# Deformable convolution, attention and experts on one core: the mean as one more column, the variance by ScalarE's squares, the output's bias added in DRAM

## The chip, the core and the metric

The kernel runs on one core of a Trainium2 chip. The metric is the device time in microseconds (us) of one execution. Five engines work side by side, each through its own queue in order: TensorE (PE in the profile, PEld its weight loads), VectorE (DVE), ScalarE (ACT), GpSimd (POOL) and SyncE (SP), which here only issues DMAs. GpSimd issues the indirect DMAs, and the one DMA that adds to what it finds in DRAM.

## The reference, cut to what matters

The input is `x[4, 256, 64, 64]`; a token is one of the 4096 pixels of one of the four images, with 256 channels.

```python
x = x + L0_conv(_gn(x), ...)            # deformable 3x3 convolution, with a residual
t = _to_tokens(x)
t = t + L1_attn(_ln_t(t), ...)          # attention over the four images; its output is o @ Wo + bo
t = t + L1_ffn(_ln_t(t), ...)           # 8 experts, the best two of a token by softmax(tokens @ router_w.T)
# _ln_t: (v - mean) / sqrt(var + 1e-5), over the 256 channels of a token
```

The attention's scores are sums over all positions, one 4x4 matrix for each of 8 heads; so they are complete only after every token has been read once.

## The kernel before, in words

Four stages follow one another.

- **Convolution** (from 0 to about 1862 us of the profiled span). For each tile of 128 pixels and each of 9 taps GpSimd gathers corners (L519), ScalarE and VectorE weigh them (L535, L543), TensorE turns and multiplies them (L557, L582). A finished row of the result `acc` has CR = 264 columns: 256 channels and 8 router columns (`NE`), the product of the row with the router's weights, since the convolution's weights have been multiplied by the router beforehand (`routed`). ScalarE copies it to `o`, and a DMA writes 4 tiles at a time to `t1[b][j]` in DRAM: image b, block j of 512 tokens, 8 blocks.
- **Scores** (to about 2181 us). For j in 8 blocks, for b in 4 images: SP loads `bt<-t` (L739, 4 tiles of 128 tokens, three buffers), `layernorm` (L184, L185 statistics, L170 variance plus epsilon, L176 the power -0.5 on GpSimd, L188 the result), TensorE turns it (L675) and projects q and k (L686), ScalarE copies them (L744, L752), VectorE multiplies every pair of images (L759, 32 instructions in each block). The compiler's scheduler orders this stage.
- **Mixing and routing** (to about 2611 us). Function `block(j)` writes out an order by hand, and TensorE, VectorE and ScalarE keep it; GpSimd's own order is fixed by the dependencies that `in_turn` adds between its powers and its scatters. For each block: `value` and `mixed` (L686, L869, L876) weigh the value projections of the four images; `gate` (L686, ScalarE's sigmoid L881), `gated` (L898), `output` (L908, 264 columns, eight of them for the router), `residual` (DMA `dt<-t` L892 and the bias added by VectorE L893), `added` (L922 the channels, L924 the router's columns), `stats` (L935, L937, then L172 and the power L176), `shift` (L948, minus the mean times 1/sigma), `normed` (L955, L960 on ScalarE, into the tile `u`), `pick` (L973 to L991, the best two experts), `count`, `placed` (L1018 to L1030, the `slots` of each token) and `scatter` (L1039, one indirect DMA for each 128 rows, 32 for a block).
- **Experts** (to the end), with the results gathered back and added.

Within `block(j)` the end of one block and the start of the next interlock. The last of block j-1 is `shift(j-1, 3)`, then `pick`, `count`, `placed`; then come `scatter(14)` of block j-1, the power of `stats(j, 0)`, `scatter(4)`, the power of `stats(j, 1)`, `scatter(4)`, the power of `stats(j, 2)`, `scatter(5)`, the power of `stats(j, 3)`, and the remaining five scatters. The call in `stats` that fixes this on GpSimd is

```python
            in_turn(issued[-1], scattered)
            scattered.clear()
```

On ScalarE the order at the end of a block is: sigmoids of image 2, sigmoids of image 3, `normed` of images 0, 1 and 2, the eight products of the next block's `value`, `normed` of image 3.

Of the kernel before, what the change touches and what calls it, by code (L numbers as in the profile page):

```python
# [9 lines left out]
F32 = mybir.dt.float32  # L10
# [7 lines left out]
P = 128  # L18
# [11 lines left out]
NE = 8  # L30


CR = C + NE
BLK = 512
NT = BLK // P
RB = BLK // W
# [33 lines left out]
def conv_attn_moe_kernel(  # L70
# [60 lines left out]
    def load_weight(pool, ap, name):  # L131
        t = pool.tile([P, NCH, ap.shape[1]], F32, name=name)
        nc.sync.dma_start(t, ap.rearrange("(ch p) o -> p ch o", p=P))
        return t

    def routed(rows, rw, ps_turned, ps_out, pool, name):


        pr = ps_out.tile([P, len(rows), NE], F32, name=f"{name}_pr", tag="om")
        for n, w in enumerate(rows):  # L140
            tp = ps_turned.tile([P, C], F32, name=f"{name}_tp{n}", tag="tp")
            for ch in range(NCH):
                T.transpose(tp[:, ch * P : (ch + 1) * P], w[:, ch * P : (ch + 1) * P], ident)
            wT = pool.tile([P, C], F32, name=f"{name}_wT{n}", tag="sT")
            S.copy(wT, tp)
            for ch in range(NCH):
                T.matmul(
                    pr[:, n, :], wT[:, ch * P : (ch + 1) * P], rw[:, ch, :],
                    start=(ch == 0), stop=(ch == NCH - 1),
                )  # L150
        for n, w in enumerate(rows):
            V.tensor_copy(w[:, C:], pr[:, n, :])
# [9 lines left out]
                reason="order of issue",  # L162
            )

    def rstd_of(pool, var, n, name, twice=False, into=None):


        ve = pool.tile([P, n], F32, name=f"{name}_ve", tag=f"ve{n}")
        if twice:
            V.tensor_scalar(ve, var, 1.0 + EPS, EPS * EPS, ALU.mult, ALU.add)  # L170
        else:
            V.tensor_scalar(ve, var, EPS, None, ALU.add)  # L172
        r = into
        if into is None:
            r = pool.tile([P, n], F32, name=f"{name}_rstd", tag=f"rstd{n}")
        issued.append(G.tensor_tensor(r, ve, nhalf[:, :n], ALU.pow))  # L176
        return r

# [23 lines left out]
    with ExitStack() as actx:  # L202
# [48 lines left out]
        wconv_sb = aw.tile([P, NCH, K2, CR], F32, name="wconv_sb")  # L251
        for ch in range(NCH):
            nc.sync.dma_start(wconv_sb[:, ch, :, :C], w_conv[ch * P : (ch + 1) * P])
        rwc_sb = load_weight(aw, router_w, "rwc_sb")


        zeros = aw.tile([P, 4 * C], F32, name="zeros")
# [436 lines left out]
    dw = wctx.enter_context(tc.tile_pool(name="d_w", bufs=1))  # L694
    wv_sb = load_weight(dw, wv, "wv_sb")
    wg_sb = load_weight(dw, wg, "wg_sb")
    rw_sb = load_weight(dw, router_w, "rw_sb")
    wo_sb = dw.tile([P, NCH, CR], F32, name="wo_sb")
    nc.sync.dma_start(wo_sb[:, :, :C], wo.rearrange("(ch p) o -> p ch o", p=P))
    bo_sb = dw.tile([P, CR], F32, name="bo_sb")  # L700
# [5 lines left out]
    with ExitStack() as bctx:  # L706
        bw = bctx.enter_context(tc.tile_pool(name="b_w", bufs=1))
        bt = bctx.enter_context(tc.tile_pool(name="b_t", bufs=3))
        bs = bctx.enter_context(tc.tile_pool(name="b_s", bufs=2))
        bqk = bctx.enter_context(tc.tile_pool(name="b_qk", bufs=2 * B + 3))  # L710
        ps_tp = bctx.enter_context(tc.tile_pool(name="ps_tpb", bufs=3, space=PSUM))
        ps_mm = bctx.enter_context(tc.tile_pool(name="ps_mmb", bufs=4, space=PSUM))

        wq_sb = load_weight(bw, wq, "wq_sb")
        wk_sb = load_weight(bw, wk, "wk_sb")
        with ExitStack() as ectx:
            et = ectx.enter_context(tc.tile_pool(name="e_t", bufs=1))
            ps_e = ectx.enter_context(tc.tile_pool(name="ps_e", bufs=1, space=PSUM))
            routed([wo_sb[:, ch, :] for ch in range(NCH)], rw_sb, ps_tp, ps_e, et, "wo")

            alike = et.tile([P, NCH, P], F32, name="alike")
            V.tensor_copy(alike, bo_c.unsqueeze(2).to_broadcast([P, NCH, P]))
            pb = ps_e.tile([P, 2, NE], F32, name="pb", tag="om")
            for n in range(2):
                for ch in range(NCH):
                    T.matmul(
                        pb[:, n, :], alike[:, ch, :] if n == 0 else ones, rw_sb[:, ch, :],
                        start=(ch == 0), stop=(ch == NCH - 1),
                    )
            V.tensor_copy(bo_sb[:, C:], pb[:, 0, :])  # L730
            V.tensor_copy(rsum, pb[:, 1, :])
        head_sum = block_diagonal(bw, "head_sum", DHEAD, 1.0)
        parts = bw.tile([P, NCH, B * B, NBLK], F32, name="parts")

        for j in range(NBLK):
            qs, ks = [], []
            for b in range(B):
                rows = bt.tile([P, NT, CR], F32, name=f"bt{b}_{j}", tag="t")
                nc.sync.dma_start(rows, t1[b][j])  # L739
                t = rows[:, :, :C]  # L740
                layernorm(bs, t, t, f"l1_{b}_{j}", twice=True)
                mn = channel_major(b, j)
                for ch, tp in transpose_in(ps_tp, t, f"tpb{b}_{j}"):
                    S.activation(  # L744
                        mn[:, ch, :], tp, AF.Identity,
                        scale=gamma_c[:, ch : ch + 1], bias=beta_c[:, ch : ch + 1],
                    )
                q = bqk.tile([P, NCH, BLK], F32, name=f"q{b}_{j}", tag="qk")
                k = bqk.tile([P, NCH, BLK], F32, name=f"k{b}_{j}", tag="qk")
                for w, dst, n in ((wq_sb, q, "q"), (wk_sb, k, "k")):  # L750
                    for ch in range(NCH):
                        S.copy(dst[:, ch, :], project(ps_mm, w, mn, ch, f"p{n}{b}_{j}_{ch}"))  # L752
                qs.append(q)
                ks.append(k)
            for s_ in range(B):
                for t_ in range(B):
                    for ch in range(NCH):
                        junk = bs.tile([P, BLK], F32, name=f"junk{s_}{t_}{ch}_{j}", tag="junk")
                        V.scalar_tensor_tensor(  # L759
                            junk, qs[s_][:, ch, :], 1.0, ks[t_][:, ch, :],  # L760
                            ALU.mult, ALU.mult,
                            accum_out=parts[:, ch, s_ * B + t_, j : j + 1],
                        )


        per_ch = bw.tile([P, NCH, B * B], F32, name="per_ch")
        V.tensor_reduce(per_ch, parts, AX.X, ALU.add)
        pl = ps_mm.tile([P, NCH * B * B], F32, name="pl", tag="mm")
        T.matmul(pl, head_sum, per_ch.rearrange("p ch n -> p (ch n)"), start=True, stop=True)
        rows = NCH * B  # L770
        lg = bw.tile([P, rows, B], F32, name="lg")
        V.tensor_scalar(lg, pl.rearrange("p (r t) -> p r t", t=B), ATT_SCALE, None, ALU.mult)
        mx = bw.tile([P, rows], F32, name="mx")
        V.tensor_reduce(mx, lg, AX.X, ALU.max)
        V.tensor_tensor(
            lg, lg, mx.unsqueeze(2).to_broadcast([P, rows, B]), ALU.subtract
        )
        S.activation(lg, lg, AF.Exp)
        V.tensor_reduce(mx, lg, AX.X, ALU.add)
        V.reciprocal(mx, mx)  # L780
        V.tensor_tensor(
            att.rearrange("p ch s t -> p (ch s) t"), lg,
            mx.unsqueeze(2).to_broadcast([P, rows, B]), ALU.mult,
        )
# [65 lines left out]
    with ExitStack() as bctx:  # L850
# [36 lines left out]
        def residual(j, b):  # L887
            for i in range(0, NT, 2):
# [1 line left out]
                    [P, 2, CR], F32, name=f"dt{b}_{j}_{i}", tag="t", bufs=4  # L890
                )
                nc.sync.dma_start(t, t1[b][j][:, i : i + 2])  # L892
                V.tensor_tensor(t, t, bo_sb.unsqueeze(1).to_broadcast([P, 2, CR]), ALU.add)  # L893

        def gated(j, b):
            o, g = os_[j, b], gs.pop((j, b))
# [16 lines left out]
        def added(j, b):  # L913
            r = token_major(b, j)
            if b == 0:
                ss[j] = bs.tile([P, NG, NE], F32, name=f"s{j}", tag="s")
                lns[j] = tuple(
                    bs.tile([P, NG], F32, name=f"{n}{j}", tag=n) for n in ("rstd", "shift")
                )
# [8 lines left out]
                nc.sync.dma_start(t2[b, j], r)  # L928

        def stats(j, b):  # L930
            x_ = token_major(b, j)
            st = bs.tile([P, NT, V.BN_STATS_DIM], F32, name=f"l3st{b}_{j}", tag="ln_st")
            mv = bs.tile([P, NT, V.BN_AGGR_DIM], F32, name=f"l3mv{b}_{j}", tag="ln_mv")
            for i in range(NT):
                V.bn_stats(st[:, i, :], x_[:, i, :])  # L935
            for i in range(NT):
                V.bn_aggr(mv[:, i, :], st[:, i, :])  # L937
            rstd_of(
                bs, mv[:, :, 1], NT, f"l3_{b}_{j}", into=lns[j][0][:, b * NT : (b + 1) * NT]
            )  # L940
            in_turn(issued[-1], scattered)
            scattered.clear()
            lns[j, b] = mv

        def shift(j, b):
            r, nb = (x[:, b * NT : (b + 1) * NT] for x in lns[j])
            mv = lns.pop((j, b))
            V.scalar_tensor_tensor(nb, mv[:, :, 0], -1.0, r, ALU.mult, ALU.mult)  # L948

        def normed(j, b):  # L950
            x_ = token_major(b, j)
            r, nb = lns[j]
            u = us[j, b] = bu.tile([P, NT, ROW], F32, name=f"u{b}_{j}", tag="u")

            S.activation(  # L955
                u[:, :, C:], place, AF.Copy, bias=float((b * HB + j % HB) * BLK)
# [10 lines left out]
        def pick(j):  # L967


            r, nb = lns.pop(j)  # L970
            lg = ss.pop(j)
            mean = bs.tile([P, NG, NE], F32, name=f"mean{j}", tag="lg", bufs=1)
            V.tensor_tensor(mean, over_tiles(rsum), over_experts(nb), ALU.mult)  # L973
            V.tensor_tensor(lg, lg, over_experts(r), ALU.mult)
# [514 lines left out]
```

## Time and profile before

| | us |
|---|---|
| median of 3 runs | 3274.14 (3273.08 to 3282.42) |
| profiled execution, its own time | 3278.02 |
| its span, first to last instruction | 3276.30 |
| busy: PE, DVE, ACT, POOL | 2972.6, 2600.0, 1722.3, 1854.4 |
| mean granted TensorE clock | 0.958 of full speed |

The profile is of one execution. Busy shares are over the whole span, in which the four stages have different limits, so the stages are read one at a time. The idle time of an engine is named by what ended it. POOL's indirect DMAs show as about 1 us of GpSimd each: that is the issue, not the transfer.

### The profile page before, as it was taken

The page shows a single profiled execution, that of the slowest core. Times are in us where ns is not written, and L with a number is a line of the kernel's source. Part 1 is how long each engine was busy: PE and PEld are TensorE (multiplying, and loading weights), DVE is VectorE, ACT ScalarE, POOL GpSimd, SP SyncE. Part 2 cuts the span into 40 slices and gives each one's busy share as a digit, 9 for nine tenths or more (in the row PEclk, how much of TensorE's full clock was granted, in tenths as well). Part 3 has the DMA queues.
Part 4 walks back from the last instruction along what each step waited for, and adds up shares of the span by engine and source line. Part 5 has one row for each costly group of instructions (what it writes and reads, how often), then busy time and mean ns, then how long its engine had stood idle before and what let it go on. Part 6 is the DMA issues. An engine that isn't in the chain of part 4 may idle for free. (4 is left out here: it accounts for less than half of the span.)

```text
span 3276.3 us, 49563 instructions
## 1 busy us (share of the span) xinstructions
PE 2972.6 (91%) x13658; PEld 2175.3 (66%) x13658; DVE 2600.0 (79%) x6611; ACT 1722.3 (53%) x3912; POOL 1854.4 (57%) x1800
## 2 busy tenths in 40 slices
PE   6889998899998899989999898978888899999995
PEld 2667776677776677767777644434444488888883
DVE  1488888878897888899999788878888766567777
ACT  3456665556664566655555444334242355556552
POOL 0377667676676767677777411105676767554440
PEclk8799999999998999999999899989999999999995
DMA  5789999999999899999999821106453445447778
GB/s 167 261 330 405 390 386 345 400 340 386 390 351 393 336 402 386 386 342 409 409 404 402 312 66 55 60 24 200 156 173 104 136 137 169 159 159 248 245 236 316
DMA packets 322182, 898.89 MB, mean 274 GB/s; under 512 B 43218, under 2 KB 89949, under 8 KB 319860
## 3 DMA queue, kind: packets, MB, share of 16 engines
q0 software_dynamic: 191808, 671.74, 53.1%
q1 hardware_dynamic: 130100, 223.98, 21.1%
q8 instruction: 113, 1.85, 0.2%
q14 instruction: 161, 1.32, 0.1%
HBM read 744.43 MB, written 154.79 MB: 274 GB/s over the span
## 5 line engine op out<-in xcount | busy, mean ns | idle before, releaser
L543 DVE SCALAR_TENSOR_TENSOR s<-g,wts,s 128x256 f32<-128x256 f32 x3456 | 1446.5, 480 | 226.4 <-ACT s L535 220.2
L519 POOL DMA_INDIRECT g<-table,idx x1152 | 1220.6, 1060 | 536.7 <-DVE s L543 279.7
L582 PE MATMUL acc<-wconv_sb,sT 128*128 128x264 f32 x4608 | 1275.2, 400 | 58.6 <-ACT sT L563 57.7
L582 PEld LDWEIGHTS acc<-wconv_sb,sT 128*128 128x128 f32 x4608 | 794.2, 192 | 186.6 <-ACT sT L563 83.9
L535 ACT ACTIVATE s<-g,wts 128x256 f32<-128x256 f32 x1152 | 587.5, 510 | 342.1 <-DMA g<-table,idx 322.4
L563 ACT COPY sT<-tps 128x256 f32<-128x256 f32 x1152 | 418.8, 364 | 352.9 <-PE tps L557 347.5
L557 PE MATMUL tps<-ident,s 128*128 128x128 f32 x2304 | 449.1, 277 | 48.6 <-DVE s L543 48.0
L557 PEld LDWEIGHTS tps<-ident,s 128*128 128x128 f32 x2304 | 316.3, 144 | 260.6 <-issue 170.9
L1313 POOL DMA_INDIRECT ys_rows<-y,to x284 | 282.7, 995 | 259.6 <-DVE y L1310 191.5
L1039 POOL DMA_INDIRECT xs_rows<-u,slots x256 | 260.6, 1018 | 126.8 <-issue 110.7
L1284 PE MATMUL ph<-xT,w 128*128 128x256 f32 x1136 | 270.8, 381 | 0.7 <-ACT hT L1288 0.6
L1302 PE MATMUL py<-w,hT 128*128 128x256 f32 x1136 | 268.4, 379 | 0.0
L1288 ACT ACTIVATE hT<-ph,w 128x256 f32<-128x256 f32 x284 | 134.4, 474 | 198.0 <-PE ph L1284 197.5
L1302 PEld LDWEIGHTS py<-w,hT 128*128 128x128 f32 x1136 | 215.8, 190 | 29.3
L1307 DVE TENSOR_TENSOR y<-py,w 128x512 f32<-128x512 f32 x142 | 98.2, 692 | 171.0 <-ACT w L1246 129.8
L1284 PEld LDWEIGHTS ph<-xT,w 128*128 128x128 f32 x1136 | 206.2, 192 | 24.1 <-ACT hT L1288 1.6
L390 PE MATMUL po<-xs,woff_sb 128*96 128x512 f32 x384 | 204.3, 628 | 0.0
L176 POOL TENSOR_TENSOR l_rstd<-l_ve,nhalf 128x4 f32<-128x4 f32 x32 | 34.4, 1075 | 253.7 <-DVE l_ve L170 253.7
L881 ACT ACTIVATE gate<-pg,bg_c 128x512 f32<-128x512 f32 x64 | 43.9, 686 | 243.0 <-PE pg L686 242.9
L759 DVE SCALAR_TENSOR_TENSOR junk<-q,k 128x512 f32<-128x512 f32 x256 | 160.9, 684 | 8.9 <-ACT k L752 8.9
L876 DVE SCALAR_TENSOR_TENSOR mix<-pv,att,mix 128x512 f32<-128x512 f32 x192 | 129.7, 742 | 1.9 <-PE pv L686 1.9
L908 PE MATMUL po<-wo_sb,mix 128*128 128x264 f32 x512 | 117.8, 386 | 0.0
(228 smaller groups left out, 3287.8 us busy)
## 6 DMA issues: line engine op xcount, KB each, us to landing
xt<-xs_rows SPq DMA_DIRECT2D x142, 260.0 KB
table<-zt SPq DMA_DIRECT2D x128, 256.0 KB
early_state<-ys_rows SPq DMA_DIRECT2D x128, 256.0 KB
g<-table,idx POOLq DMA_INDIRECT x1152, 7.8
t<-o SPq DMA_DIRECT2D x32, 528.0 KB
bt<-t SPq DMA_DIRECT2D x32, 528.0 KB
dt<-t SPq DMA_DIRECT2D x64, 264.0 KB
xraw<-in_x SPq DMA_DIRECT2D x16, 1024.0 KB
```

What stands on the lines that cost most here:

```text
L390: T.matmul(t["po"], woff_sb[:, ch, ki].rearrange("p kj o -> p (kj o)"), t["xs"][:, ch, ki : ki + RB], start=(n == 0), stop=(n == NCH * 3 - 1),
L519: g = G.indirect_dma_start(out=gs[n % NGB], out_offset=None, in_=tables[b], in_offset=bass.IndirectOffsetOnAxis(ap=params[b][0][:, r, k : ...
L535: first = S.activation(ss[n], gs[n % NGB][:, :C], AF.Copy, scale=params[b][1][:, 0, r, k : k + 1])
L543: last_corner[n] = V.scalar_tensor_tensor(ss[n], gs[n % NGB][:, c * C : (c + 1) * C], params[b][1][:, c, r, k : k + 1], ss[n], ALU.mult, A ...
L557: T.transpose(tps[n][:, ch * P : (ch + 1) * P], s[:, ch * P : (ch + 1) * P], ident)
L563: S.copy(sTs[n], tps.pop(n))
L582: T.matmul(accs[n // K2][:, :CR], sT[:, ch * P : (ch + 1) * P], wconv_sb[:, ch, k, :], start=False, stop=(k == K2 - 1 and ch == NCH - 1),)
L759: V.scalar_tensor_tensor(junk, qs[s_][:, ch, :], 1.0, ks[t_][:, ch, :], ALU.mult, ALU.mult, accum_out=parts[:, ch, s_ * B + t_, j : j + 1],)
L1039: s = G.indirect_dma_start(out=rows_, out_offset=bass.IndirectOffsetOnAxis(ap=slots[:, k, n : n + 1], axis=0), in_=u[:, n % NT, :], in_off ...
L1284: T.matmul(ph, w1_sb[:, ch, f * P : (f + 1) * P], xT[:, ch, :], start=(ch == 0), stop=(ch == NCH - 1),)
L1302: T.matmul(py[:, i, :], hT[:, f, i * P : (i + 1) * P], w2_sb[:, f, :], start=(f == 0), stop=(f == NCH - 1),)
L1313: s = G.indirect_dma_start(out=ys_rows[g], out_offset=bass.IndirectOffsetOnAxis(ap=to[:, i : i + 1], axis=0), in_=y[:, i, :], in_offset=No ...
```

## The change

The router's weights get a ninth column (`NX` = 9) filled with -1/256. A row's product with it is minus the row's mean, and it is carried wherever the eight router columns were carried: CR is 265. `stats` no longer uses VectorE's statistics: ScalarE squares each tile of 128 tokens with the carried mean as its bias and sums along the row (`accum_out`), into `u`, which `normed` overwrites later; VectorE forms variance plus epsilon from the sum. `shift` takes the mean from the ninth column. The bias `bo_sb` is no longer added by VectorE in `residual`: in the scores' loop, after a block has been loaded, GpSimd issues a DMA that adds it to `t1[b][j]` in DRAM; the load of that loop takes only the 256 channels.

```diff
-CR = C + NE
+NX = NE + 1
+CR = C + NX
...
+    def load_router(pool, name):
+        t = pool.tile([P, NCH, NX], F32, name=name)
+        G.memset(t[:, :, NE:], -1.0 / C)
+        nc.sync.dma_start(t[:, :, :NE], router_w.rearrange("(ch p) o -> p ch o", p=P))
+        return t
...
-        rwc_sb = load_weight(aw, router_w, "rwc_sb")
+        rwc_sb = load_router(aw, "rwc_sb")
...
-    rw_sb = load_weight(dw, router_w, "rw_sb")
+    rw_sb = load_router(dw, "rw_sb")
...
-                rows = bt.tile([P, NT, CR], F32, name=f"bt{b}_{j}", tag="t")
-                nc.sync.dma_start(rows, t1[b][j])
-                t = rows[:, :, :C]
+                t = bt.tile([P, NT, C], F32, name=f"bt{b}_{j}", tag="t")
+                nc.sync.dma_start(t, t1[b][j][:, :, :C])
                 layernorm(bs, t, t, f"l1_{b}_{j}", twice=True)
+                G.dma_start(
+                    t1[b][j], bo_sb.unsqueeze(1).to_broadcast([P, NT, CR]), accum_op=ALU.add
+                )
...
                 nc.sync.dma_start(t, t1[b][j][:, i : i + 2])
-                V.tensor_tensor(t, t, bo_sb.unsqueeze(1).to_broadcast([P, 2, CR]), ALU.add)
...
         def stats(j, b):
-            x_ = token_major(b, j)
-            st = bs.tile([P, NT, V.BN_STATS_DIM], F32, name=f"l3st{b}_{j}", tag="ln_st")
-            mv = bs.tile([P, NT, V.BN_AGGR_DIM], F32, name=f"l3mv{b}_{j}", tag="ln_mv")
+            x_, mean = token_major(b, j), ss[j][:, :, NE:]
+            u = us[j, b] = bu.tile([P, NT, ROW], F32, name=f"u{b}_{j}", tag="u")
+            var = bs.tile([P, NT], F32, name=f"l3var{b}_{j}", tag="var")
             for i in range(NT):
-                V.bn_stats(st[:, i, :], x_[:, i, :])
-            for i in range(NT):
-                V.bn_aggr(mv[:, i, :], st[:, i, :])
-            rstd_of(
-                bs, mv[:, :, 1], NT, f"l3_{b}_{j}", into=lns[j][0][:, b * NT : (b + 1) * NT]
+                n = b * NT + i
+                S.activation(
+                    u[:, i, :C], x_[:, i, :], AF.Square, bias=mean[:, n],
+                    accum_out=var[:, i : i + 1],
+                )
+            ve = bs.tile([P, NT], F32, name=f"l3_{b}_{j}_ve", tag=f"ve{NT}")
+            V.tensor_scalar(ve, var, 1.0 / C, EPS, ALU.mult, ALU.add)
+            issued.append(
+                G.tensor_tensor(lns[j][0][:, b * NT : (b + 1) * NT], ve, nhalf[:, :NT], ALU.pow)
             )
...
-            mv = lns.pop((j, b))
-            V.scalar_tensor_tensor(nb, mv[:, :, 0], -1.0, r, ALU.mult, ALU.mult)
+            V.tensor_tensor(nb, ss[j][:, b * NT : (b + 1) * NT, NE], r, ALU.mult)
...
-            u = us[j, b] = bu.tile([P, NT, ROW], F32, name=f"u{b}_{j}", tag="u")
+            u = us[j, b]
...
-            lg = ss.pop(j)
+            lg = ss.pop(j)[:, :, :NE]
```

Built, the changed kernel keeps the orders written by hand. On ScalarE the four squares of image 0 stand between the sigmoids of image 2 and those of image 3; the squares of images 1, 2 and 3 stand each after `normed` of the image before. On VectorE the instruction that forms the variance plus epsilon stands where it stood. On GpSimd the powers and scatters of the mixing stage stand as they stood; in the scores' stage the first two adding DMAs stand ahead of the first power, and the further ones one or two at a time between the powers.

More of the change, by code (lines that the diff above doesn't have):

```diff
@@ L134, in load_weight @@
         return t
+    def load_router(pool, name):
[3 more added lines that the diff above has]
+        return t
     def routed(rows, rw, ps_turned, ps_out, pool, name):
-        pr = ps_out.tile([P, len(rows), NE], F32, name=f"{name}_pr", tag="om")
+        pr = ps_out.tile([P, len(rows), NX], F32, name=f"{name}_pr", tag="om")
         for n, w in enumerate(rows):
@@ L163, in in_turn, with rstd_of @@
             )
-    def rstd_of(pool, var, n, name, twice=False, into=None):
+    def rstd_of(pool, var, n, name, twice=False):
         ve = pool.tile([P, n], F32, name=f"{name}_ve", tag=f"ve{n}")
@@ L172, in rstd_of @@
             V.tensor_scalar(ve, var, EPS, None, ALU.add)
-        r = into
-        if into is None:
-            r = pool.tile([P, n], F32, name=f"{name}_rstd", tag=f"rstd{n}")
+        r = pool.tile([P, n], F32, name=f"{name}_rstd", tag=f"rstd{n}")
         issued.append(G.tensor_tensor(r, ve, nhalf[:, :n], ALU.pow))
@@ L722, in conv_attn_moe_kernel @@
             V.tensor_copy(alike, bo_c.unsqueeze(2).to_broadcast([P, NCH, P]))
-            pb = ps_e.tile([P, 2, NE], F32, name="pb", tag="om")
+            pb = ps_e.tile([P, 2, NX], F32, name="pb", tag="om")
             for n in range(2):
@@ L730, in conv_attn_moe_kernel @@
             V.tensor_copy(bo_sb[:, C:], pb[:, 0, :])
-            V.tensor_copy(rsum, pb[:, 1, :])
+            V.tensor_copy(rsum, pb[:, 1, :NE])
         head_sum = block_diagonal(bw, "head_sum", DHEAD, 1.0)
@@ L915, in added @@
             if b == 0:
-                ss[j] = bs.tile([P, NG, NE], F32, name=f"s{j}", tag="s")
+                ss[j] = bs.tile([P, NG, NX], F32, name=f"s{j}", tag="s")
                 lns[j] = tuple(
@@ L942, in stats @@
             scattered.clear()
-            lns[j, b] = mv
         def shift(j, b):
             r, nb = (x[:, b * NT : (b + 1) * NT] for x in lns[j])
-            mv = lns.pop((j, b))
-            V.scalar_tensor_tensor(nb, mv[:, :, 0], -1.0, r, ALU.mult, ALU.mult)
+            V.tensor_tensor(nb, ss[j][:, b * NT : (b + 1) * NT, NE], r, ALU.mult)
         def normed(j, b):
```

## The prediction

> **What bounds the kernel now.** I read the busy time by stretches first, since the change acts in two stages. Columns: stretch, its length, busy us (and instructions) of PE, PEld, DVE, ACT and POOL, granted clock, DMA share, GB/s. The rows are the scores, the first block of mixing, the other seven blocks.
>
> ```profile
> 1870.00:2181.00 311.00, 267.48 (x779) 130.89 (x780) 259.33 (x938) 119.89 (x194) 34.91 (x35) 0.93 0.17 55
> 2181.00:2229.50 48.50, 46.18 (x135) 25.65 (x134) 38.51 (x92) 17.75 (x33) 4.17 (x3) 0.97 0.33 108
> 2229.50:2611.00 381.50, 322.87 (x932) 172.79 (x930) 324.46 (x874) 132.89 (x294) 258.03 (x244) 0.95 0.44 149
> ```
>
> No engine is full in the last row, and VectorE, at 85%, looks like the one to relieve. So I went on to the timeline of one block, for a chain that closes on itself. First GpSimd (start, length, engine, line, what it does, in brackets the idle time before it):
>
> ```profile
> 2300.90 0.95 POOL L1039 DMA_INDIRECT xs_rows<-u,slots  x1 [6.19 <-issue]
> 2302.16 0.96 POOL L1039 DMA_INDIRECT xs_rows<-u,slots  x1 [0.30 <-issue]
> ...
> 2318.59 0.96 POOL L1039 DMA_INDIRECT xs_rows<-u,slots  x1 [0.30 <-issue]
> 2319.67 1.22 POOL L176 TENSOR_TENSOR rstd<-l_ve,nhalf 128x4 f32<-128x4 f32 x1
> ...
> 2325.94 1.57 POOL L176 TENSOR_TENSOR rstd<-l_ve,nhalf 128x4 f32<-128x4 f32 x1
> ...
> 2332.60 1.22 POOL L176 TENSOR_TENSOR rstd<-l_ve,nhalf 128x4 f32<-128x4 f32 x1
> ...
> 2340.13 1.32 POOL L176 TENSOR_TENSOR rstd<-l_ve,nhalf 128x4 f32<-128x4 f32 x1
> ```
>
> Then VectorE in the same block:
>
> ```profile
> 2300.68 0.18 DVE L1030 CAST slots<-row 128x16 int32<-128x16 f32 x1
> ...
> 2319.22 0.29 DVE L172 TENSOR_SCALAR l_ve<-l3mv 128x4 f32<-128x4 f32 x1
> ...
> 2341.49 0.16 DVE L948 SCALAR_TENSOR_TENSOR shift<-l3mv,rstd 128x4 f32<-128x4 f32 x1 [0.94 <-POOL rstd L176]
> ...
> 2353.87 0.17 DVE L1030 CAST slots<-row 128x16 int32<-128x16 f32 x1
> ```
>
> The reader is to see a loop. Slots are ready at 2300.86; 14 scatters, one every 1.26 us, fill GpSimd to 2319.55; then four powers with 4, 4 and 5 scatters between them, without a gap, to 2341.45. VectorE waits for the last power, shifts, picks, mixes, and has the next slots at 2354.04. That is 40.6 us of GpSimd and 12.6 of VectorE: 53.2 us, the period of the block. VectorE is busy beside GpSimd but only 12.6 us of its work are in the loop. Its variance for the first power (L172) ends at 2319.51, 0.04 us before GpSimd is free. So an earlier variance gains nothing, a later one delays the loop.
>
> The third view is ScalarE at the end of the same block:
>
> ```profile
> 2319.18 0.69 ACT L881 ACTIVATE gate<-pg,bg_c 128x512 f32<-128x512 f32 x1 [1.03 <-PE pg L686]
> ...
> 2326.18 0.69 ACT L881 ACTIVATE gate<-pg,bg_c 128x512 f32<-128x512 f32 x1 [1.03 <-PE pg L686]
> ...
> 2326.87 2.06 ACT L960 ACTIVATE u<-early_state,shift,rstd 128x256 f32<-128x256 f32 x4
> ...
> 2336.03 4.70 ACT L869 ACTIVATE mix<-pv,att 128x512 f32<-128x512 f32 x8
> ```
>
> ScalarE is a third full, but in order: `normed` of image 0 starts only when the sigmoids of image 3 are done, and the new squares of image 1 stand behind it.
>
> **The mixing stage, blocks 1 to 7.** Removed from VectorE per block: eight adds at L893, 0.62 us apart (two in 1.24), 5 us; 16 statistics and aggregations, 1.7 us an image, 6.8 us. Of this the loop holds nothing. Two adds stand between the slots and the first power; without them VectorE, and the TensorE products that wait for its mixes, come 1.24 us earlier.
>
> Added: 16 squares on ScalarE. No row shows a square with a sum. L535, 128x256 with one operand per partition, takes 510 ns, L960 with two 588, and four L960 take 2.06, a pitch of 0.49; so a square has a pitch of 0.41. For the sum, the smallest ScalarE row (L985, four in 0.47) gives a pitch of 0.1 us. Four squares: 4 x 0.51 + 0.1, so 2.2 us; bounds 1.75 (sum free) and 3.0 (194 ns each, L985 alone, and the pitch of L960). I take 2.2, as VectorE's own read of a sum (84 ns) is nearer to the lower row. The built program has no more table loads than before (seven), so no switch is charged.
>
> Now the steps, by the block above:
> - Image 0: the sigmoids of image 2 end at 2319.87 - 1.24 = 2318.6. Squares to 2320.8, variance and hand-over 0.25, power at 2321.1 instead of 2319.67. Queued behind VectorE's waiting instruction: `gated` of image 2 and `added` of image 1.
> - Image 1: the sigmoids of image 3 end at 2325.6, `normed` of image 0 at 2327.6, squares at 2329.8, power at 2330.05 instead of 2325.94: **4.1 us late**. VectorE, done with `shift` at 2324, stands still for some 6 us, and behind it `gated` of image 3, for which TensorE waits.
> - Images 2 and 3: from power to power GpSimd needs 6.66 and 7.53 us (four and five scatters). Shift, `normed` (2.06), squares (2.2) and hand-overs need about 6.1 from power to power. GpSimd sets the pace again, with 0.5 and 1.5 us to spare, and the 4.1 us stay.
>
> With squares of 1.75 the delay is 3.7, with 3.0 it is 5.2. The next slots come as much later: nothing in the 12.6 us changed.
>
> A second cost is TensorE's clock. The eight products at L869 start behind the squares of image 3, at 2342.4, so TensorE, with three of four value projections done by 2340.5, idles to about 2344.7, some 4.2 us. After an idle time of 3.94 us the trace shows eight matmuls (L686, 512 columns) at 6.03 us, which take 3.60 later:
>
> ```profile
> 1875.98 2.19 PE L675 MATMUL tpb<-ident,bt 128*128 128x128 f32 x8 [3.94 <-DVE bt L188]
> 1878.46 6.03 PE L686 MATMUL pq<-early_state,wq_sb 128*128 128x512 f32 x8 [0.29 <-ACT early_state L744]
> 1884.32 3.60 PE L686 MATMUL pk<-early_state,wk_sb 128*128 128x512 f32 x8
> ```
>
> That is up to 2.4 us more before the products that `placed` needs, which had some 2.4 us to spare and lose about 2 of it: 0 to 2.2 us a block, I take 0.5. The Trainium skill ("TensorE: Matmul & The Clock Gate", Part 1) speaks against this change here: after an idle window of about 3.4 us the array runs at half clock for about as long again; by it the sum would have 1.7 us a block instead of 0.5, 8 us more in all.
>
> Seven blocks: 7 x (4.1 + 0.5) = 32.2 us. In block 0 nothing is scattered, and powers follow each other after 4.83 us (2225.89, 2230.72) where the new chain needs 6.0: three steps, 3.5 us. **Sum 35.7 us**; bounds 28 (3.7 a block and 2) and 56 (7.4 and 4).
>
> **The scores' stage.** GpSimd gets 32 adding DMAs. No row shows one. A gather of 128 rows costs GpSimd 1060 ns; this one has 512 rows, so 1.06 to 4.24 us, and I take 2.6, between them, as a part of the 1060 must be fixed. Two of them precede the first power and wait for `bo_sb`, written at 1872.25: with 0.3 us between issues the power moves from 1874.44 to 1878.1, 3.5 us (0.6 to 7). Later VectorE sets the pace, 36.3 us a block (powers at 1931.67 and 1967.93), and an issue fits between two powers 4.43 us apart up to 3.4 us: 0.5 us in all, at most 7. The transfer is covered: DMA share is 0.17, and GpSimd waits for the landing only eight such DMAs later. The load it follows, 540 KB, is issued at 1888.82 and used at 1892.47, 3.65 us. Read, read and write one after another make 11 us at most. I take **4 us** for the stage, 0.6 to 15. The Trainium skill ("DMA: Bandwidth & Descriptors", Anatomy of one DMA) gives 2.0 us plus bytes/436e3 for a DMA from GpSimd, 3.2 us for this one, not for one that adds; by it the transfer would be hidden even more surely.
>
> **The convolution.** One more column: 16 matmuls of 264 columns take 3.72 us, 8 of 512 take 3.60, so 0.84 ns a column, times 4608, 3.9 us if TensorE set the pace. ScalarE waited 322 us there for gathers, and DMA share is 0.97 to 1.00 between 200 and 1800 us, so most of it is covered: **1 us**, 0 to 4. The ninth column elsewhere, the memsets and the copies: nothing, a few ns each.
>
> **Sum.** 3278.0 (the profiled execution; 1.7 of it outside the span) + 35.7 + 4 + 1 = 3318.7. That execution lies 3.9 above the median, so 3315 in the median's terms, 41 us slower (1.2%).
>
> **Rivals.**
> - *VectorE sets the pace and its relief pays.* For it: 85% busy, and GpSimd waited 9.9 us for the variance in 2230 to 2611. Against: the loop above. If squares ran beside everything, 12 us a block would go, 8 x 12 = 97: 3274 - 97 + 5 = 3182; with GpSimd's loop as floor only the 9.9 and some 5 of block 0 go: 3264. It decides if the variance of image 1 is ready within 25 us of the slots, instead of 29. Chance 0.08.
> - *Squares in time, loop unchanged*: sigmoids of image 3 earlier than I have them. 3274 + 5, less a few of the 9.9: 3274. Chance 0.07.
> - *The adding DMAs become the bound of the scores' stage.* An image has 9.07 us there (36.3/4). At 11 us each, the end above, 1.9 x 32 = 61 us more: 3376, and worse beyond it. Against: DMA share 0.17. Chance 0.15.
> - The forecast: 0.70, 3296 to 3336 by itself.
>
> The range reaches from the lower bounds (3302), with some room, to part of the third rival: 3296 to 3358. The measurement can tell 0.3% (9.8 us) from no change. Faster 0.08, same 0.07, slower 0.85.
>
> **What would show it.** Right: blocks 1 to 7 some 58 to 60 us apart instead of 53 to 55; VectorE idle some 6 us ahead of the variance of image 1, put down to ScalarE; that power some 29 us behind the slots; no gap on GpSimd after it; the scores' stage longer by a few us. Wrong: GpSimd still without a gap before the second power (faster or same), squares over 0.8 us apart (block by more than 6), or GpSimd at over 4 us an adding DMA, VectorE waiting for loads or powers in the scores.

## The result, and the profile after

The change makes the kernel slower: 3303.3 us (median of four runs) against 3274.1, a ratio of 1.0084 with a 95% interval of 1.0055 to 1.0112. The forecast was 3315, in a range from 3296 to 3358. The profiled execution of the changed kernel took 3301.75 us (span 3300.0), 23.7 more than the one of before; that one lies 3.9 above its kernel's median and this one 1.5 below, so the stages below account for 23.7 us, not for the 29 between the medians.

I read the stages first, by the same instructions in both kernels. The convolution ends where GpSimd clears `head_sum`; the scores end with ScalarE's first mix; the mixing stage goes from there to the start of the last power.

| stage | predicted | before | after | difference |
|---|---|---|---|---|
| convolution | +1 | 1861.2 | 1855.8 | -5.4 |
| scores | +4 | 322.8 | 328.0 | +5.2 |
| mixing and routing | +35.7 | 431.7 | 452.1 | +20.4 |
| rest, to the end | 0 | 660.6 | 664.0 | +3.4 |

Busy time by stretches, columns as in the prediction (PE, PEld, DVE, ACT, POOL, granted clock, DMA share, GB/s), for the scores, the first block of mixing and the other seven:

```profile
1870.00:2181.00 311.00, 267.14 (x771) 129.28 (x772) 258.16 (x917) 119.83 (x194) 71.75 (x65) 0.93 0.58 105
2181.00:2229.50 48.50, 43.55 (x121) 23.77 (x120) 26.30 (x52) 21.75 (x52) 2.89 (x3) 0.92 0.29 94
2229.50:2631.00 401.50, 330.40 (x947) 182.63 (x945) 245.16 (x597) 190.05 (x521) 245.74 (x244) 0.95 0.42 143
```

VectorE was relieved as intended: in the seven blocks it is busy 245 us instead of 324. The stage is longer all the same. One block of it, as in the prediction, GpSimd first:

```profile
2361.95 0.95 POOL L1050 DMA_INDIRECT xs_rows<-u,slots  x1 [6.39 <-issue]
...
2382.02 1.34 POOL L952 TENSOR_TENSOR rstd<-l_ve,nhalf 128x4 f32<-128x4 f32 x1 [2.65 <-DVE l_ve L950]
...
2391.03 1.41 POOL L952 TENSOR_TENSOR rstd<-l_ve,nhalf 128x4 f32<-128x4 f32 x1 [2.64 <-DVE l_ve L950]
...
2397.50 1.04 POOL L952 TENSOR_TENSOR rstd<-l_ve,nhalf 128x4 f32<-128x4 f32 x1
...
2404.85 1.04 POOL L952 TENSOR_TENSOR rstd<-l_ve,nhalf 128x4 f32<-128x4 f32 x1
```

The first two powers now have a gap ahead of them, the last two have none. VectorE of the same block:

```profile
2361.73 0.17 DVE L1041 CAST slots<-row 128x16 int32<-128x16 f32 x1
...
2381.70 0.17 DVE L950 TENSOR_SCALAR l_ve<-l3var 128x4 f32<-128x4 f32 x1 [4.28 <-ACT u L945]
...
2390.78 0.17 DVE L950 TENSOR_SCALAR l_ve<-l3var 128x4 f32<-128x4 f32 x1 [6.28 <-ACT u L945]
...
2405.92 0.16 DVE L959 TENSOR_TENSOR shift<-s,rstd 128x4 f32<-128x4 f32 x1 [2.85 <-POOL rstd L952]
...
2418.41 0.17 DVE L1041 CAST slots<-row 128x16 int32<-128x16 f32 x1
```

VectorE stands still 4.28 and 6.28 us for ScalarE's squares. Why they are late is to be seen on ScalarE: the squares of image 1 (L945) stand behind the sigmoids of image 3 (L890) and `normed` of image 0 (L971).

```profile
2386.03 0.69 ACT L890 ACTIVATE gate<-pg,bg_c 128x512 f32<-128x512 f32 x1 [0.97 <-PE pg L692]
2386.61 0.20 ACT L966 ACTIVATE u<-place 128x16 f32<-128x16 f32 x1
2386.72 2.06 ACT L971 ACTIVATE u<-early_state,shift,rstd 128x256 f32<-128x256 f32 x4
2388.68 0.49 ACT L945 ACTIVATE u<-early_state,s 128x256 f32<-128x256 f32 x1
2389.08 0.19 ACT L945 ACTIVATION_READ_ACCUMULATOR u<-early_state,s 128x1 f32 x1
2389.18 0.49 ACT L945 ACTIVATE u<-early_state,s 128x256 f32<-128x256 f32 x1
```

From the slots (2361.90) to the end of the fourth power (2405.89) are 44.0 us, from there to the next slots 12.7; the block takes 56.7.

### The profile page after: what moved, and what is told of

Its sections match the earlier page's. It is cut to its first block, busy times and chain, and to the rows that moved or that the text cites. A ratio compares the mean times of both kernels' runs of the same rounds, so it can differ in the third digit from the quotient of the medians.

```text
span 3300.0 us, 49621 instructions
## 1 busy us (share of the span) xinstructions
PE 2978.9 (90%) x13658; PEld 2177.2 (66%) x13658; DVE 2507.8 (76%) x6291; ACT 1784.4 (54%) x4168; POOL 1865.9 (57%) x1834
## 3 DMA queue, kind: packets, MB, share of 16 engines
q0 software_dynamic: 208704, 689.10, 56.7%
q14 instruction: 161, 1.32, 0.1%
## 5 line engine op out<-in xcount | busy, mean ns | idle before, releaser
L525 POOL DMA_INDIRECT g<-table,idx x1152 | 1207.7, 1048 | 544.3 <-DVE s L549 291.9
L588 PE MATMUL acc<-wconv_sb,sT 128*128 128x265 f32 x4608 | 1274.6, 399 | 57.0 <-ACT sT L569 55.5
L1050 POOL DMA_INDIRECT xs_rows<-u,slots x256 | 250.8, 980 | 128.4 <-issue 127.2
L916 PE MATMUL po<-wo_sb,mix 128*128 128x265 f32 x512 | 137.9, 428 | 31.2 <-DVE s L932 31.2
L890 ACT ACTIVATE gate<-pg,bg_c 128x512 f32<-128x512 f32 x64 | 44.0, 687 | 202.0 <-PE pg L692 202.0
L916 PEld LDWEIGHTS po<-wo_sb,mix 128*128 128x128 f32 x512 | 108.5, 214 | 66.6 <-issue 44.1
```

The source lines that it names most:

```text
L525: g = G.indirect_dma_start(out=gs[n % NGB], out_offset=None, in_=tables[b], in_offset=bass.IndirectOffsetOnAxis(ap=params[b][0][:, r, k : ...
L588: T.matmul(accs[n // K2][:, :CR], sT[:, ch * P : (ch + 1) * P], wconv_sb[:, ch, k, :], start=False, stop=(k == K2 - 1 and ch == NCH - 1),)
L916: T.matmul(po[:, n, :CR], o[:, ch, (i + n) * P : (i + n + 1) * P], wo_sb[:, ch, :], start=(ch == 0), stop=(ch == NCH - 1),)
L1050: s = G.indirect_dma_start(out=rows_, out_offset=bass.IndirectOffsetOnAxis(ap=slots[:, k, n : n + 1], axis=0), in_=u[:, n % NT, :], in_off ...
```

## The experiments

They ran on three other chips (the first four on one, the next four on another, the last four on a third), on which the kernel before took 3590 to 3631 us. Most of that excess is in the convolution, which ends at 2120 to 2191 us there. Ratios are therefore taken to runs of the kernel before on the same chip, and stages are compared, as far as possible, among runs of one chip; executions of one kernel differ there by 1.3 to 1.6%.

**The two halves apart.** e1 gives the variance back to VectorE and keeps the rest; e2 gives the bias back to VectorE and keeps the rest.

```diff
 # e1, in stats
-                S.activation(u[:, i, :C], x_[:, i, :], AF.Square, bias=mean[:, n],
-                             accum_out=var[:, i : i + 1])
+                V.bn_stats(st[:, i, :], x_[:, i, :])      # then bn_aggr, as before
 # e2, in the scores' loop and in residual
-                G.dma_start(t1[b][j], bo_sb..., accum_op=ALU.add)
+                V.tensor_tensor(t, t, bo_sb.unsqueeze(1).to_broadcast([P, 2, CR]), ALU.add)
```

> The changed kernel, with the variance taken by VectorE's statistics again; the ninth column, the mean from it and the bias added in DRAM stay. My theory (ScalarE's squares, in order behind sigmoids and normed, make the loop through GpSimd longer): the second power of a block is back at about 25 us behind the slots (29.1 in the changed kernel, 25.1 before), GpSimd has no gap ahead of it, the blocks lie 53 to 54 us apart (56.7 and 54.9), the scores' stage stays 5 us longer; 3265 to 3276 us, within 0.3% of before. Rival (the adding DMAs in DRAM, or the ninth column, are what costs): the time stays near 3300, with the blocks still 56 us apart or the cost in the scores' stage.

Measured: 1.0012 of before (0.9981 to 1.0042). The mixing stage takes 431.1 us; GpSimd has no gap ahead of the second power in six of the seven blocks. The rest of the expectation failed: the blocks are 55.5 us apart, and the second power comes 24.9 to 28.1 us behind the slots, because in four blocks GpSimd now waits 3.6 to 4.2 us ahead of the first power, as in block 4:

```profile
2727.32 1.34 POOL L950 TENSOR_TENSOR rstd<-l_ve,nhalf 128x4 f32<-128x4 f32 x1 [3.63 <-DVE l_ve L948]
```

The last section comes back to this wait.

> The changed kernel, with the bias added by VectorE in the mixing stage as before and no adding DMA; squares and ninth column stay. My theory: the squares carry the loss; the scores' stage is back at 323 us (328 in the changed kernel), but VectorE's two adds per image come back, two of them between the slots and the first power, so the first power comes about 1.2 us later still: 3300 to 3312 us. Rival (the DRAM adds carry the loss): 3274 to 3282.

Measured: 1.0123 (1.0074 to 1.0171), the slowest of these four and a little over what was expected (about 1.008 to 1.012). The mixing stage takes 485.8 us.

So the squares carry the loss. The move of the bias by itself (with the ninth column) cannot be told from no change. Whether the mixing stage gains by it what the scores' stage loses is not shown: there is no profile of the kernel before on this chip.

**The adding DMAs alone.** e3 leaves the adding DMAs out, and with them the bias (zeros in these inputs).

```diff
-                G.dma_start(t1[b][j], bo_sb..., accum_op=ALU.add)
```

> The changed kernel without the 32 adding DMAs, and without the bias, which is zero in these inputs. It prices them alone. My theory: only the scores' stage changes, from 328 back to about 323 us, most of it ahead of its first power, and the DMA share there falls from 0.58 to about 0.17: 3296 to 3300 us. Rival (the adding DMAs' traffic or their place in GpSimd's queue costs in the mixing stage too): under 3290, with blocks nearer than 56 us.

Measured: 1.0066 (1.0039 to 1.0093), and 461.0 us for the mixing stage. Against e2, which differs from it only in VectorE's adds, 24.8 us are gone: 3.1 us a block, more than the 1.24 that I had counted for the two adds between the slots and the first power. The steps behind it are longer too: 6.85 and 8.05 us in e2, 6.47 and 7.38 in e3. In the first of them GpSimd stands 0.39 us ahead of the third power, in the second the third power itself takes 1.43 us where e3 has 1.04. Against e1, which has statistics in the place of the squares, the mixing stage is 29.9 us longer in e3 on the same chip, though e3 has no adding DMA. The scores' stage takes 325.0 us. Over all runs it takes 327.1 to 330.3 with the adding DMAs (nine profiles) and 322.5 to 325.0 without (five): 4.7 us between the means.

The profile shows where these are not: the first power is no later. The time from the clearing of `head_sum` to it is 13.2 us before and after. GpSimd issues the first two adding DMAs ahead of it in 2.57 us, while it would have waited for the variance anyway:

```profile
1867.20 2.57 POOL L748 DMA_DIRECT2D t<-bo_sb  x2 [10.38 <-DVE l_st L190]
1869.09 1.76 POOL L182 TENSOR_TENSOR l_rstd<-l_ve,nhalf 128x4 f32<-128x4 f32 x1
...
1967.95 1.24 POOL L748 DMA_DIRECT2D t<-bo_sb  x1 [0.33 <-issue]
```

More than half of them are in the first two blocks: from the first power to the fourth of the second block are 60.4 us instead of 57.2 (58.5 to 60.9 in the nine profiles with adding DMAs, 56.6 to 57.4 in the five without). VectorE waits 8.7 us for loads there instead of 6.6. The other six blocks take 36.6 us each instead of 36.2. A part of it shows in the groups of VectorE's instructions in 1870 to 2200 us (busy us, mean ns of one, then the idle time before them), first of before, then of after: the normalisation takes 424 ns instead of 409, up to 577 where GpSimd issues an adding DMA beside it.

```profile
L188 DVE TENSOR_SCALAR bt<-bt,l_mv,l_rstd 128x256 f32<-128x256 f32 x128 | 45.5, 409 | 32.4 <-POOL l_rstd L176 32.4
```
```profile
L194 DVE TENSOR_SCALAR bt<-bt,l_mv,l_rstd 128x256 f32<-128x256 f32 x128 | 47.4, 424 | 33.7 <-POOL l_rstd L182 30.9 <-PE pq L692 1.5 <-PE tpb L681 1.2
```

That makes VectorE's work 1.9 us longer over the stage; how much of it lies on the path is not shown.

**The order on ScalarE.** e4 moves one step, e7 two.

```diff
 # e4
-            normed(j, 0)
             squares(j, 1)
+            normed(j, 0)
 # e7: the same, and the sigmoids of images 2 and 3 taken out of gate()
             squares(j, 0)
+            sigmoids()          # those of image 2
...
             squares(j, 1)
+            sigmoids()          # those of image 3
             shift(j, 0)
             normed(j, 0)
```

> The changed kernel with one step moved on ScalarE: the squares of image 1 stand ahead of normed of image 0 instead of behind it. My theory (the order on ScalarE delays the second power): that power comes 2.06 us earlier, 27 us behind the slots, GpSimd's gap ahead of it shrinks from 2.64 to 0.6 us, the blocks come 2 us closer (54.6 instead of 56.7), 14 us in seven blocks: 3287 to 3291 us. Rival (the squares are late because their data come late from TensorE and VectorE, or the delay is made up or lost elsewhere): no change against 3303, within 3 us.

> The changed kernel once more, on the same chip as the next three, so that their stages can be compared with its own. Against before: 1.006 to 1.011 in any theory. Where the chip is like that of the first four experiments, my reading of those says that its blocks are 57 to 58 us apart, with GpSimd waiting 5 to 6 us ahead of the first power of a block (2.65 in the first profile of this kernel) and less ahead of the second (0.5 instead of 2.64); if the adding DMAs had moved that wait, it stays at 2.65 and 2.64 here.

> The kernel before once more, for its stages on this chip: the scores' stage 5 to 7 us shorter than in the changed kernel beside it, the seven blocks 53 to 55.5 us apart. My theory: the difference of the two kernels lies in the first power to last power of the mixing stage (15 to 25 us) and in the scores' stage (5 to 7), and the convolution and the experts differ by no more than runs of one kernel do. Rival: the ninth column costs in the convolution, or the experts are longer in the changed kernel, by over 3 us again.

> The changed kernel with ScalarE's order moved twice: the squares of image 0 ahead of the sigmoids of image 2, and those of image 1 ahead of the sigmoids of image 3 and of normed of image 0. My theory (the squares are late only because they stand behind other work of ScalarE): the first power loses its 1.3 us of delay and the second its 4 us, the steps between powers are GpSimd's own (6.1 to 6.5, 6.5, 7.4), the blocks are 53 to 54 us apart, and 20 to 28 us of the loss come back: 0.999 to 1.003 of before. Rival (the sigmoids, now later, delay gated, TensorE's output and with them images 2 and 3 by as much): blocks 56 us apart or more, 1.006 or more.

Measured: e4 1.0048 (1.0012 to 1.0083), e5 (the changed kernel again) 1.0051 (1.0016 to 1.0087), e7 1.0009 (0.9978 to 1.0040). The times of e4 and e5 cannot be told apart (they ran on two chips); the powers can. The first and second power of block 1, in e5, in e4 and in e7:

```profile
2578.06 1.41 POOL L952 TENSOR_TENSOR rstd<-l_ve,nhalf 128x4 f32<-128x4 f32 x1 [1.33 <-issue]
2587.15 1.41 POOL L952 TENSOR_TENSOR rstd<-l_ve,nhalf 128x4 f32<-128x4 f32 x1 [2.65 <-DVE l_ve L950]
```
```profile
2539.48 1.41 POOL L958 TENSOR_TENSOR rstd<-l_ve,nhalf 128x4 f32<-128x4 f32 x1 [1.33 <-issue]
2546.50 1.41 POOL L958 TENSOR_TENSOR rstd<-l_ve,nhalf 128x4 f32<-128x4 f32 x1 [0.57 <-issue]
```
```profile
2582.99 1.06 POOL L964 TENSOR_TENSOR rstd<-l_ve,nhalf 128x4 f32<-128x4 f32 x1
2589.09 1.32 POOL L964 TENSOR_TENSOR rstd<-l_ve,nhalf 128x4 f32<-128x4 f32 x1
```

They are 9.09 us apart in e5 (and in e3, on e4's chip), 7.02 in e4 (2.07 less, as computed) and 6.10 in e7, which here has no gap ahead of either. In five of the seven blocks of e5 GpSimd waits some 6 us ahead of the first power instead of 2.65; then mostly only 0.5 us of waiting is left ahead of the second, and e4 ends its fourth power only 0.9 us nearer to the slots in such blocks. Its mixing stage takes 449.6 us against 461.0 in e3 on the same chip.

e7 takes away the delay of the second power (0.46 us of it stay in one block), that of the first in two blocks. In the other five GpSimd still waits 4.6 to 4.9 us ahead of the first power, as in block 3:

```profile
2694.95 1.04 POOL L964 TENSOR_TENSOR rstd<-l_ve,nhalf 128x4 f32<-128x4 f32 x1 [4.64 <-DVE l_ve L962]
```

Its mixing stage is 440.5 us against 459.3 in e5 on the same chip, 18.8 less, and the step to its last power keeps GpSimd's own pace. By time alone e5 and e7 are not clearly apart, for their intervals overlap. The blocks are 56.6 us apart, not the 53 to 54 expected (58.8 in e5, 55.8 in e6, the kernel before). The rival's spacing (56 or more) came, its cause did not: images 2 and 3 are not held up, for the third power follows the second as closely as in e5 in six blocks and the fourth follows in all seven, and the time is 1.0009 where the rival asked for 1.006.

e5 and e6 also say what of the first pair of profiles repeats. The mixing stage is 459.3 against 438.6 us, 20.7 longer (20.4 on the first chip). That the totals agree so well is in part chance: e5 waits longer ahead of its first powers, e6 has gaps of 2.3 to 3.1 us ahead of the second power in three blocks, and on the first chip neither is so. The scores' stage is 2.5 longer (5 to 7 expected). The convolution is 24.5 shorter and the rest 10.3 shorter in the changed kernel: there single executions scatter by more than the change could do, and neither the 5.4 us gained nor the 3.4 lost on the first chip is an effect of it that I could show.

**GpSimd's queue.** e8 is e1 with three of the scatters moved from ahead of the fourth power to behind it.

```diff
             stats(j, 2)
-            scatter(5)
+            scatter(2)
```

> The variance by VectorE's statistics, the bias added in DRAM (as e1), and two scatters instead of five between the third and the fourth power; the other three go out behind it, where GpSimd stands idle 6.4 us. My theory (GpSimd's queue up to the fourth power is the loop that bounds a block): the fourth power comes 3.8 us earlier, the blocks are 50 to 51.5 us apart, 18 to 26 us less than e1: 0.993 to 0.997 of before. Rival (VectorE or TensorE sets the block as soon as GpSimd is a little faster): the fourth power waits for its variance instead, blocks as in e1, 1.000 of before.

Measured: 0.9952 (0.9923 to 0.9981), by the ratio 17 us faster than before: on its chip this version beats both kernels. The mixing stage takes 417.3 us, 21.3 less than in e6 on the same chip. The third and the fourth power of block 2:

```profile
2635.84 1.04 POOL L950 TENSOR_TENSOR rstd<-l_ve,nhalf 128x4 f32<-128x4 f32 x1
2640.33 1.04 POOL L950 TENSOR_TENSOR rstd<-l_ve,nhalf 128x4 f32<-128x4 f32 x1 [0.94 <-DVE l_ve L948]
```

They are 4.49 us apart instead of 7.37 in e1. The fourth power waits 0.94 us for its variance: GpSimd was the bound, and 2.9 us further on VectorE is. From the first power of block 1 to that of block 7 are 321.8 us against 332.8 in e1 (on another chip): 1.8 us a block, less than the 2.9, and the blocks are 53.6 us apart on average, not the 50 to 51.5 expected.

**One step further, and too far.** e9, e10 and e12 deal the scatters out 16, 2, 2, 2 and 10: on the kernel before, on e1 and on e7. e11 is e7 once more, for comparison on that chip.

```diff
-            scatter(14)
+            scatter(16)
...          # and scatter(2) between the powers
```

> The kernel before with the scatters of a block dealt out otherwise: 16 ahead of the first power and two between the powers, ten behind the last, instead of 14, 4, 4, 5 and 5. Nothing of the change is in it. My theory (GpSimd's queue up to the fourth power bounds a block of the kernel before): the powers come as soon as VectorE has the variances, 5.5 to 6.2 us apart instead of 6.3, 6.7 and 7.5, the blocks 51 to 53 us apart instead of 53 to 56: 0.993 to 0.998 of before. Rival (the loads that VectorE's bias adds wait for, or TensorE, set the block): 0.999 to 1.002.

> The variance by VectorE's statistics and the bias added in DRAM (as e1), with the scatters dealt out 16, 2, 2, 2 and 10. My theory: with GpSimd out of the way the steps between powers are those of VectorE's chain (shift, added, statistics), 4.5 us each as the last step of e8 was; a block loses another 3 us against e8: blocks 49 to 51 us apart, 0.988 to 0.992 of before. Against e9 the missing adds on VectorE bring 1.2 us per image and the adding DMAs cost 5 us in the scores' stage. Rival (TensorE, busy some 45 us of a block, becomes the bound): steps of 4.5 but blocks of 52 to 53 us as in e8, 0.995.

> Placeholder order of e7 on this chip, for its stages beside those of the other runs: the changed kernel with the sigmoids of images 2 and 3 behind the squares of images 0 and 1, scatters as in the changed kernel. Blocks 53 to 57 us apart, the first power of a block on time or late with TensorE, the second with GpSimd; 1.000 of before.

> The changed kernel with ScalarE's order as in e7 and the scatters dealt out 16, 2, 2, 2 and 10, so that neither ScalarE's other work nor GpSimd's queue is ahead of the squares. My theory: squares on ScalarE still lose to statistics on VectorE, since between two powers stand shift, normed (2.06), squares (2.06) and two hand-overs on one engine, about 6.1 us: steps of 6.1 us instead of 4.5, blocks 3 to 5 us further apart than in e10, 0.996 to 1.000 of before. Rival (the place of the statistics does not matter once GpSimd is out of the loop): blocks and time as e10, within 0.3%.

Measured: e9 1.0102 (1.0054 to 1.0150), e10 1.0187 (1.0132 to 1.0243), e12 1.0170 (1.0110 to 1.0230). My expectations of their times all failed, and the comparison of statistics with squares that they were meant for cannot be made. The mixing stage takes 493.6, 487.4 and 499.1 us, in e11 with its 14 scatters 442.3 (3640.2 us in its one run, 1.003 of the median of before). e10's last step is 4.49 us as expected, e9's 4.87 in five blocks (5.5 to 6.2 expected), but the first power of a block now waits up to 16 us. The timeline of e10 between slots and powers shows who is missing (PE is TensorE; "remote" means that the profile found no releaser on this core's engines):

```profile
2690.17 1.98 PE L692 MATMUL pv<-early_state,wv_sb 128*128 128x512 f32 x4 [1.14 <-issue]
...
2692.80 1.98 PE L692 MATMUL pg<-early_state,wg_sb 128*128 128x512 f32 x4 [0.65 <-issue]
...
2696.39 0.75 DVE L885 SCALAR_TENSOR_TENSOR mix<-pv,att,mix 128x512 f32<-128x512 f32 x1 [3.64 <-remote]
2704.11 0.75 DVE L885 SCALAR_TENSOR_TENSOR mix<-pv,att,mix 128x512 f32<-128x512 f32 x1 [6.97 <-issue]
...
2711.87 0.69 ACT L890 ACTIVATE gate<-pg,bg_c 128x512 f32<-128x512 f32 x1 [28.49 <-remote]
...
2712.61 3.78 PE L692 MATMUL pg<-early_state,wg_sb 128*128 128x512 f32 x4 [17.82 <-ACT gate L890]
```

VectorE and ScalarE get the results of products recorded at 2690 to 2695 only at 2696.39, 2704.11 and 2711.87, 7.7 us from one to the next. Up to 2708 us GpSimd issues scatters, 26 in a row with hardly a pause, and from 2680 us on DMA share is 0.28 to 0.32; then both stop, and the last late result follows. In block 1, where no scatters come from a block before, the first power of e9, e10 and e12 waits for nothing. Long unbroken runs of scatters thus go with late results of TensorE; by what path was not found out.

## Why the prediction was right, and where its sizes were not

- **The loop and its delay: right.** The first power stands 20.1 us behind the slots (18.8 before, 1.4 later predicted), the second 29.1 (29 predicted, 25.1 before), VectorE waits 6.28 us for the squares of image 1 (6 predicted), GpSimd has no gap after that. The four squares take 2.06 us with their sums (2.2 taken). e1 shows that the squares are the cause; e4 and e7 show that for the second power it is their place in ScalarE's order. Those runs are from other chips, none from the first.
- **The size of the mixing stage: 35.7 us predicted, 20.4 measured.** That lies under the term's own lower bound of 28, so part of the hit is luck: the range had room below. Two steps failed. First, 4.1 + 0.5 us a block were added to a loop of 53.2, but the block that I had taken was the shortest; the seven periods between first powers sum to 382.2 us before, 54.6 on average. In three other blocks the first power already waited 1.31 us for its variance (2.52 in a fourth), the last step took 7.9 to 8.0 us in four, and one period, that from block 4 to block 5, is 58.7 us. The first power of block 3 before:

```profile
2374.54 1.34 POOL L176 TENSOR_TENSOR rstd<-l_ve,nhalf 128x4 f32<-128x4 f32 x1 [1.31 <-DVE l_ve L172]
```

  After they sum to 398.9, or 57.0: 2.4 a block. The rest of the 20.4 lies ahead of the first power of block 0 (1.4) and behind that of block 7 (2.3). Second, the delay of the second power does not stay whole. With VectorE idle the last two powers take 1.04 us where they took 1.22 and 1.32, the steps 6.47 and 7.35 instead of 6.66 and 7.53, so the loop to the end of the fourth power grows by 3.4 (44.0 against 40.6), not by 4.1.
- **Block 0: 3.5 us predicted, 2.95 measured, by luck.** I took three steps of 4.83 us, but only the last of the three is so short; the first two powers before:

```profile
2212.98 1.38 POOL L176 TENSOR_TENSOR rstd<-l_ve,nhalf 128x4 f32<-128x4 f32 x1 [33.66 <-DVE l_ve L172]
2218.97 1.39 POOL L176 TENSOR_TENSOR rstd<-l_ve,nhalf 128x4 f32<-128x4 f32 x1 [4.61 <-DVE l_ve L172]
```

  The steps are 5.99, 6.92 and 4.83 us before and 9.08, 5.99 and 5.62 after, 2.95 more together: the first is now as long as in the later blocks, the second is shorter.
- **TensorE's clock: 0.5 us a block predicted, none in the loop.** TensorE does wait and then does run slowly: the output of image 3 takes 5.50 us after an idle time of 3.91, where the others take 3.74; the granted clock is 0.69 of full speed over it and 1.00 over the output before it.

```profile
2385.83 3.74 PE L916 MATMUL po<-wo_sb,mix 128*128 128x265 f32 x16
2393.48 5.50 PE L916 MATMUL po<-wo_sb,mix 128*128 128x265 f32 x16 [3.91 <-DVE s L932]
```

  That idle time is not where I had put it: ahead of the last value products, where 4.2 us were predicted, TensorE waits 1.1 us, because it is late itself by then. And VectorE's part of the loop is 12.7 us, as before. The Trainium skill's rule ("TensorE: Matmul & The Clock Gate", Part 1) agrees with these rows as to the clock; the 1.7 us a block that I had estimated by it do not appear in the loop's period, since VectorE's part of the loop is no longer.
- **Scores' stage: 4 us predicted, 5.2 measured (4.7 over all profiles), by another path, so the agreement is luck.** The issue of an adding DMA takes 1.2 us, not 2.6. I had counted it on top of the first power's time, 3.5 us, though GpSimd waited 12 us for the variance there: it delays that power by nothing. The first two blocks become 3.2 us longer and the six others 0.4 us each, where I had 0.5 in all; the end of the stage is 0.5 us shorter. The transfer lands 6.6 us after its issue. The Trainium skill ("DMA: Bandwidth & Descriptors", Anatomy of one DMA) led to an estimate of 3.2 us for one that does not add. DMA share in the stage goes from 0.17 to 0.58; in the last six blocks the loads stay hidden as forecast, in the first two VectorE waits 2.1 us more for them. The rival in which the adding DMAs become the bound did not come.
- **Convolution: 1 us predicted.** A product of 265 columns takes 399 ns, one of 264 took 400: no cost can be seen.
- **The rivals with a gain** needed the second variance by 25 us behind the slots. It came at 29. In e7 it holds GpSimd up no longer, and the time is that of before within its interval, as the second rival had it.

## What to carry to other kernels

Before work moves to an emptier engine, find its place in that engine's order: here 2 us of squares had their data and stood for 4 us behind other work of that engine, and the engine that was relieved only waited. Price a change in a loop against the mean of its rounds rather than the clearest one. A bound that is not busy all the time, here GpSimd's queue up to its last power, may be relieved by moving three instructions into its own idle time, and the same move taken further can cost more than it gave.

## What I had not expected of the hardware

- On three of the four chips TensorE's results can reach their readers late while GpSimd issues indirect DMAs in long runs. In e3, with 14 scatters in a row, the first half of this product is recorded to end about 2646.1, and ScalarE's sigmoid gets it 4.4 us later (in the changed kernel on the first chip 0.04 us later):

```profile
2644.25 3.60 PE L692 MATMUL pg<-early_state,wg_sb 128*128 128x512 f32 x8
2650.50 1.27 ACT L887 ACTIVATE gate<-pg,bg_c 128x512 f32<-128x512 f32 x2 [8.94 <-PE po L913]
```

  So it is, by 4.3 to 4.6 us, in five or six of the seven later blocks of e1, e3, e4 and e5, and in four of e8; with it go most of the waits of 3.6 to 6.3 us ahead of the first power in those runs. In e2 and e6, where VectorE adds the bias as before, the sigmoids of this image are late by 1.5 us once and by 0.6 to 2.4 us in five blocks; why is not shown. With 26 scatters in a row the first power waits up to 16 us (e10). The records show no wait of TensorE that would explain it, and in such a stretch of e5 (2672 to 2697 us) no transfer of instructions. The convolution, which issues 1152 gathers, is 260 to 330 us longer on these chips. What it is stays open.
- A power of 128 x 4 values on GpSimd takes 1.04 us while VectorE is idle and up to 1.58 in the kernel before while it works, though not every time. The other way round, VectorE's normalisation of 128 x 256 takes 409 ns on average before, and up to 577 beside the issue of an adding DMA.
- Reading a sum on ScalarE is recorded as an instruction of 0.19 us of its own, of which about 0.1 adds to the pitch: a square with its sum comes every 0.49 us, and its read begins 0.40 after it.
